# Chain steps in every cell, another softmax for the third unit, and two held pairs of V in a two-block attention kernel

## The chip, the core and the metric

The kernel runs on one core of a Trainium2 chip. The metric is device time in microseconds (us), lower is better. A core has a matmul engine (TensorE, PE in the profile; its weight loads are shown as PEld), a vector engine (VectorE, DVE), an activation engine (ScalarE, ACT), a general engine (GpSimd, POOL) and a queue engine that starts DMAs (SyncE, SP). [...]

## What is computed

Two transformer blocks, one after the other, on x of shape (2, 1024, 256) in fp32, with 16 heads of 16. Both attend to themselves and then to a context of 64 rows for each batch. The first ends with a mixture of 8 experts (two for each row), the second with a plain feed-forward layer. Cut to what matters:

```python
# block 0
q = ln(x);  x = x + mha(q, q)                 # self attention, 1024 keys
x = x + mha(ln(x), ln(ctx))                   # cross attention, 64 keys
h = ln(x);  vals, idx = top_k(h @ rw.T + rb, 2)
x = x + sum_k softmax(vals)[k] * expert[idx[k]](h)   # gelu, 256 -> 1024 -> 256
# block 1
x = x + mha(ln(x), ln(x))
x = x + mha(ln(x), ctx, bias=-10000 * (1 - mask))
x = x + ff(ln(x))                             # gelu, 256 -> 1024 -> 256
```

Each attention is softmax(q k^T / 4) v, with the maximum of each row subtracted.

## The kernel before

**Self attention** of a block (`self_attention`) is a loop over cells. A head group of four heads with 512 queries is eight cells; there are 16 groups (2 batches, 2 halves of the queries, 4 groups of heads), so 128 cells. In cell c four matmuls of kind "a" (L806) make scores for cell c + 10 (`LEAD`) whose row maxima VectorE takes (L813), and four of kind "b" (L817) make the scores of cell c again, transposed and with the maxima subtracted, whose exponentials ScalarE takes (L823). The products with V (`product`, L868) follow every second cell, or a cell alone. `has_a` and `maxima[0]` say that maxima are still to be made: cells 0 to 117. The last cells have "b" alone. The maxima of a group are collected by `collect` (L841), transposed on PE (L714) and subtracted from the queries (L716) in `largest`. `need_heads` forces out, with `stream.until`, the projections of keys and queries (`keys`, `queries`, L636), whose results go through DMAs on SP into the tiles KS and QS, that the next "a" needs.

**All else in the loop** is a task of a planner, `Stream`. A task is a generator: it emits instructions and yields a cost in us of PE time. A cost of zero or less means "not before the next cell" (or so many cells of 2.9 us, `CELL`). A task has a due cell (`last`), a first cell, marks that it waits for (`after`) and a rank. Each cell adds `pace` to an allowance `owed`: at least `RATE`, 2.5 us in block 0 and 1.1 us in block 1, and more when due times need it. Then `stream.step` takes the able task that is due first, and of equals (most have no due time) the one of the highest rank, until the allowance or 3 us are spent. After the loop, `rest` runs what is left by rank, with a model of time for the waits.

**A unit** is 512 rows, of which there are four. When its self attention is finished, `project` adds it to x (two halves, L438 and L446) and calls `when_ready`, which adds the unit's chain by `cross_tasks`: the norm of four row tiles (`norm_task`), the cross attention `weigh` (query projections L1114; then steps), and `share` (the projection). In block 0 the routing of the unit follows (`dispatch_task`: top two experts, places, and eight indirect DMAs on POOL that scatter its rows, L1474), then a search for the experts' tiles (`Mixture.find`), and slots of 256 rows for an expert (`Mixture.slot`). Slot 0 needs the routing of two units, slots 1 to 4 that of three, the others of all four.

**The steps of `weigh`** work on a group g of heads and a row of the group r: scores (SC, L1148), subtraction of the maximum (LA, L1168 and L1169), masks in block 1 (MA), exponentials (EX, L1185), division by the sum (DI, L1191 to L1193), transposes (TU, L1201) and products (PR, L1215). If the unit begins while maxima are made (`whole`), all these are laid out over 19 cells (21 in block 1). Otherwise the exponential is taken as the transposes are copied out, and the sums are made by products: `undivided` (products L1230, sums L1240, reciprocals L1249) and `division` (L1255, L1262). In block 1 the masks are then added by PE (L1139), unless scores were made while maxima are.

**The lead-in** of block 0 makes maxima of ten cells before the loop. At each of its ten points it adds 1.4 us to an allowance; after the eighth it collects the first maxima, fills up with tasks, and transposes them. V is made in four pairs of row tiles (`values`, L606), due in cells 0, 2, 4 and 6.

Of the kernel before, what the change touches and what calls it, by code (L numbers as in the profile page):

```python
# [61 lines left out]
LEAD = 10  # L62
# [59 lines left out]
class Task:  # L122

    def __init__(self, steps, cost, first=-99, last=None, mark=None, after=(), rank=0):
        self.steps, self.left, self.first = steps, cost, first
        self.soft, self.last = last is None, 9999 if last is None else last
        self.mark, self.after, self.rank = mark, after, rank


class Stream:
# [20 lines left out]
    def step(self, cell):  # L153
        while True:
            able = [t for t in self.tasks if t.first <= cell and self.made.issuperset(t.after)]
            if not able:
                return None
            cost = self.advance(min(able, key=lambda t: (t.last, -t.rank)), cell)
            if cost and cost > 0.0:
                return cost  # L160

    def pace(self, cell):

# [39 lines left out]
def two_blocks(  # L203
# [109 lines left out]
    maxima = [True]  # L313
# [163 lines left out]
    whole = tc.dram_tile([NPAIR, 2 * P, 512], F32, name="whole")  # L477
# [49 lines left out]
    def self_attention(layer, tail, heads, arrive, extra, when_ready, beside=None):  # L527
# [89 lines left out]
            free.append(i)  # L617
            yield 2.0

        def add_values(b, first, after):  # L620

            for c0 in range(0, TB, 2):
                stream.add(
                    values(b, c0), 2.0, first=first, last=64 * b + c0, mark=("values", b, c0),
                    after=after if c0 == 0 else [("values", b, c0 - 2)],
                )

# [160 lines left out]
        def project(b, qh, after=()):  # L788
            def go():
                for t0 in range(0, 4, 2):  # L790
                    yield from project_task(ot[b, qh], w, b * TB + 4 * qh + t0, t0, 2)
                when_ready(b, qh, stream, now[0])

            stream.add(go(), 4.0, last=now[0] + 4, rank=60, after=after)

        def score(kind, cell, j):
            h, n = divmod(cell, 8)
# [125 lines left out]
            opool, qpool = results_pool(), weights_pool()  # L923
            stream.made.add(("QB", 0))
        stream.made.update([("norm", 0), ("Q", 0)])
        add_values(0, -99, [("norm", 0)])
        add_heads(2)
        add_heads(4)
        add_heads(6)
# [30 lines left out]
        for cell in range(ncell + 2):  # L960
            now[0] = cell
            ahead = cell + LEAD
            if ahead < ncell and ahead % 16 == 0:
                need_heads(ahead // 8)
            has_a, has_b = ahead < ncell, cell < ncell
            maxima[0] = has_a
            a = [("a", ahead, j) for j in (2, 3, 0, 1)] if has_a else []
            s = [("b", cell, j) for j in range(4)] if has_b else []
            if has_a:
                slot(s[:2] + a[:2])  # L970
                slot(s[2:] + a[2:])
            elif has_b:
                slot(s)
            if ahead % 8 == 7 and has_a:
                h = ahead // 8
                collect(h)
                stream.add(largest(h), 0.75, first=cell + 1, last=cell + 2, mark=("QB", h))
            if (cell + 1) % 8 == 0 and cell + 1 < ncell:
                stream.until(("QB", (cell + 1) // 8))
            for go in later.pop(cell, []):  # L980
                go()
            owed = min(owed, 3.0) + max(stream.pace(cell), 0.0 if has_a else 2.0)
            if cell >= 2 and cell % 2 == 0:
                product([c for c in (cell - 2, cell - 1) if c not in alone])
                if owed < 2.5:
                    continue
            most = 3.0
            while owed > 0.6 and most > 0.0:
                cost = stream.step(cell)
                if cost is None:  # L990
                    break
                owed -= cost
                most -= cost

            if cell % 2 == 1 and most > 2.0 and cell < ncell:
                alone.add(cell - 1)
                product([cell - 1])
# [79 lines left out]
    def cross_tasks(stream, layer, n, pool, first):  # L1077


        att = 2 * layer + 1  # L1080
        w = weights[att]
        b, t0 = n // 2, 4 * n
        name = f"c{layer}{n}"
        held = {}
# [10 lines left out]
        stream.add(  # L1095
            weigh(layer, b, pool, w, name, held), 17.0,
            mark=("weighed", n), after=[("cnorm", n), before[0]], rank=30,
        )
        stream.add(
            share(w, name, t0, held), 5.0, mark=("cross", n),  # L1100
            after=[("weighed", n)], rank=50,
        )

    def weigh(layer, b, pool, w, name, held):

        att = 2 * layer + 1
        kbd, vbd = kbds[layer], vbds[layer]
# [3 lines left out]
        for g in range(2):  # L1111
            i, p = bank()
            for k in range(2):
                nc.tensor.matmul(  # L1114
                    p,
                    lhsT=w[:, X_Q + k * D + g * P : X_Q + k * D + (g + 1) * P],
                    rhs=xT[:, k, :],
                    start=(k == 0),
                    stop=(k == 1),
                )  # L1120
            nc.scalar.activation(
                q[:, g, :], p, AF.Identity, bias=cols[:, C_Q[att] + g : C_Q[att] + g + 1]
            )
            free.append(i)
            yield 1.72
        shape = [P, 4 * 2, SK]
        less, pts, whole_scores = {}, {}, set()


        whole = maxima[0]  # L1130

        def scores(g, n):

# [139 lines left out]
        if whole:  # L1273
# [16 lines left out]
            for now in cells:  # L1290
# [5 lines left out]
                if now is not cells[-1]:  # L1296
                    yield 0.0 if maxima[0] else -1.5
            return
        for step, *args, wait in (
            (SC, 0, 0, None),  # L1300
            (SC, 0, 1, -1.0),
            (TU, 0, 0, None),
            (SC, 1, 0, None),
            (TU, 0, 1, -1.3),
            (undivided, 0, None),
            (SC, 1, 1, None),
            (TU, 1, 0, None),
            (division, 0, None),
            (TU, 1, 1, -1.6),
            (undivided, 1, None),  # L1310
        ):
            step(*args)
            yield costs[step]
            if wait:
                yield wait

    def share(w, name, first, held):

        if held["division"]:
            yield -2.6  # L1320
            held["division"](1)
            yield 0.55
        yield -1.2
        for t0 in range(0, 4, 2):
            yield from project_task(held["ot"], w, first + t0, t0, 2)


    inside = const.tile([P, E], F32, name="inside")
# [869 lines left out]
```

## Time and profile before

| | us |
|---|---|
| median of three runs | 1615.26 (1612.68 to 1616.85) |
| the profiled execution | 1614.59 |
| its span, first to last instruction | 1612.8 |
| PE busy | 1560.5 (97%) |
| DVE busy | 1013.8 (63%) |
| ACT busy | 939.3 (58%) |
| POOL busy | 472.2 (29%) |

By the timeline the span falls into: the lead-in to about 50 us, block 0's loop with maxima to 529, its last cells to 577, the chains of the last units and the first slots to about 656, the other slots to about 948, block 1's loop to 1402, its last cells to 1430, and the rest with the feed-forward layer to the end.

A line of the profile names a line of the kernel, an engine, an operation, and output and inputs by the program's names. A group's line ends with its busy time, the mean of one in ns, and the idle time in front of it with what ended it. In the view of waits the numbers are the total, how often, and the longest. In the page's slices a digit is tenths of a fortieth of the span (40.3 us). PEclk is the granted clock of PE. A matmul in fp32 shows as two records, so a pass of four matmuls has "x8".

### The profile page before, as it was taken

What the parts mean: (1) busy time and instruction counts of PE and PEld (TensorE: products, weight loads), DVE (VectorE), ACT (ScalarE), POOL (GpSimd) and SP (SyncE); (2) the same over time, 40 slices, a digit from 0 to 9 for tenths busy, and PEclk for the clock granted to TensorE, in tenths of its full rate; (3) what the DMA queues carried; (4) which work ended last, traced back from release to release, by engine and by line L of the source; (5) the groups of instructions that cost most, each with busy time, mean ns of one, the idle gap of its engine ahead of it and who ended that gap; (6) DMA issues with size and microseconds to landing.
All of it is one profiled execution on the core that took longest, in us unless ns stands there. A gap on an engine that the chain in (4) does not pass through costs nothing. (4 is left out here: it accounts for less than half of the span.)

```text
span 1612.8 us, 27523 instructions
## 1 busy us (share of the span) xinstructions
PE 1560.5 (97%) x10182; PEld 853.7 (53%) x10182; DVE 1013.8 (63%) x2178; ACT 939.3 (58%) x1821; POOL 472.2 (29%) x589
## 2 busy tenths in 40 slices
PE   7999999999999888899999999999999999999998
PEld 3533443443444356688888753344344444446766
DVE  5788776877878856511114458876777878845400
ACT  3488777866867752332333337876777877864321
POOL 2234333433623302311112032411333525511000
PEclk9899999998999999999999999999999999999999
DMA  5236211100100214475656321101110001000000
GB/s 157 113 134 226 81 34 29 34 14 21 41 25 18 67 49 134 153 272 189 203 190 234 92 73 28 35 21 22 34 34 21 22 27 70 22 28 1 14 13 26
DMA packets 55749, 120.98 MB, mean 75 GB/s; under 512 B 12218, under 2 KB 26428, under 8 KB 55228
## 3 DMA queue, kind: packets, MB, share of 16 engines
q1 hardware_dynamic: 51772, 109.02, 21.0%
q0 software_dynamic: 3456, 9.51, 1.6%
q8 instruction: 82, 1.34, 0.3%
q10 hardware_dynamic: 384, 0.66, 0.2%
q14 instruction: 55, 0.45, 0.1%
HBM read 71.64 MB, written 38.88 MB: 69 GB/s over the span
## 5 line engine op out<-in xcount | busy, mean ns | idle before, releaser
L813 DVE TENSOR_REDUCE mx_s<-banks 128x1 f32<-128x512 f32 x1024 | 633.2, 680 | 187.0 <-PE banks L806 182.5
L823 ACT ACTIVATE pt_s<-banks 128x512 f32<-128x512 f32 x1024 | 532.9, 611 | 134.8 <-PE banks L806 107.0
L806 PE MATMUL banks<-KS,QS 16*128 16x512 f32 x2048 | 535.0, 631 | 0.2 <-issue 0.2
L817 PE MATMUL banks<-qb_s,KS 32*128 32x512 f32 x2048 | 516.5, 624 | 7.2 <-DVE qb_s L716 2.3
L881 POOL TENSOR_TENSOR acc_s<-acc_s,part_s 128x512 f32<-128x512 f32 x151 | 191.6, 1269 | 370.3 <-ACT part_s L880 369.2
L817 PEld LDWEIGHTS banks<-qb_s,KS 32*128 32x128 f32 x2048 | 179.3, 187 | 194.5 <-DVE mx_s L813 116.3
L868 PE MATMUL banks<-pt_s,v_s 128*20 128x512 f32 x2048 | 265.8, 604 | 2.6 <-DVE mx_s L813 1.9
L806 PEld LDWEIGHTS banks<-KS,QS 16*128 16x128 f32 x2048 | 199.1, 185 | 64.9 <-issue 29.5
L1731 PE MATMUL banks<-w_slot,h_s 128*128 128x256 f32 x640 | 145.2, 384 | 0.0
L868 PEld LDWEIGHTS banks<-pt_s,v_s 128*20 128x20 f32 x2048 | 42.4, 98 | 191.7 <-ACT pt_s L823 142.9
L1731 PEld LDWEIGHTS banks<-w_slot,h_s 128*128 128x128 f32 x640 | 121.7, 192 | 20.4 <-DVE mx_s L813 1.5
L1740 DVE SCALAR_TENSOR_TENSOR ys<-banks,gate,b 128x256 f32<-128x256 f32 x40 | 19.3, 483 | 172.0 <-PE banks L1731 167.7
L880 ACT COPY part_s<-banks 128x512 f32<-128x512 f32 x166 | 100.3, 605 | 45.8 <-PE banks L868 41.3
L1746 POOL DMA_INDIRECT results<-ys,to x40 | 38.7, 967 | 261.5 <-DVE ys L1740 183.2
L1707 ACT ACTIVATE h_s<-banks,w_slot 128x256 f32<-128x256 f32 x104 | 43.6, 470 | 111.3 <-issue 64.0
L1701 PE MATMUL banks<-xsT,w_slot 128*128 128x256 f32 x416 | 96.2, 383 | 0.9 <-ACT xsT L377 0.9
L1701 PEld LDWEIGHTS banks<-xsT,w_slot 128*128 128x128 f32 x416 | 78.0, 191 | 15.4 <-DVE mx_s L813 2.3
L636 PE MATMUL banks<-xT_s,w_att 128*128 128x512 f32 x128 | 63.9, 635 | 0.5 <-DVE mx_s L813 0.5
L1864 ACT ACTIVATE h_f<-banks,w_ff 128x512 f32<-128x512 f32 x32 | 22.0, 687 | 69.7 <-PE banks L1861 69.7
L1873 PE MATMUL banks<-w_ff,h_f 128*128 128x256 f32 x256 | 57.3, 380 | 0.0
L1707 ACT ACTIVATE h_s<-banks,spare 128x256 f32<-128x256 f32 x56 | 23.5, 470 | 57.3 <-issue 33.4
L1861 PE MATMUL banks<-hT_f,w_ff 128*128 128x512 f32 x128 | 56.8, 594 | 0.0
(282 smaller groups left out, 1666.0 us busy)
## 6 DMA issues: line engine op xcount, KB each, us to landing
w_slot<-in_ff_w_dram SPq DMA_DIRECT2D x40, 576.0 KB
sorted_rows<-fill SPq DMA_DIRECT2D x36, 520.0 KB
w_slot<-in_ff_w_dram SPq DMA_DIRECT2D x26, 514.0 KB
whole<-acc_s SPq DMA_DIRECT2D x30, 256.0 KB
spare<-in_ff_w_dram SPq DMA_DIRECT2D x14, 514.0 KB
xs<-sorted_rows SPq DMA_DIRECT2D x20, 260.0 KB
y<-results SPq DMA_DIRECT2D x16, 256.0 KB
QS<-stq_s SPq DMA_DIRECT2D x124, 32.0 KB
```

The costliest lines, as they stand in the source:

```text
L636: nc.tensor.matmul(p, lhsT=w[:, at + k * D + pair * P : at + k * D + (pair + 1) * P], rhs=xT[b][:, k, blk * 512 : (blk + 1) * 512], start= ...
L806: nc.tensor.matmul(sc, lhsT=QS[h % 4][r, qc * P : (qc + 1) * P], rhs=K[r, kh * 512 : (kh + 1) * 512], start=True, stop=True,)
L813: return i, lambda: nc.vector.tensor_reduce(mx[h][:, qc, j, kh : kh + 1], sc, AX.X, ALU.max)
L817: nc.tensor.matmul(sc, lhsT=K[r, n * P : (n + 1) * P], rhs=QB[h][r, :], start=True, stop=True)
L823: nc.scalar.activation(pt, sc, AF.Exp, scale=SCALE)
L868: nc.tensor.matmul(o[32 * j : 32 * j + VW, :], lhsT=V[b][:, cell % 8, 4 * g + j, :], rhs=exps.pop((cell, j)), start=(cell == cells[0]), st ...
L880: nc.scalar.copy(part, o)
L881: helper().tensor_tensor(acc[h], acc[h], part, ALU.add)
L1701: nc.tensor.matmul(ph[:, n, :], lhsT=w[:, at : at + P], rhs=xT[:, k, :], start=(k == 0), stop=(k == 1),)
L1707: nc.scalar.activation(h1[:, f, :], ph[:, n, :], AF.Gelu, bias=w[:, W_B1 + f : W_B1 + f + 1])
L1731: nc.tensor.matmul(py, lhsT=h1[:, f, h * P : (h + 1) * P], rhs=w[:, f * D : (f + 1) * D], start=(f == 0), stop=(f == 7),)
L1873: nc.tensor.matmul(py[:, n, :], lhsT=h1[:, f, t * P : (t + 1) * P], rhs=w2[:, f * D : (f + 1) * D], start=(f == 0), stop=(f == 7),)
```

## The change

It has four parts. (1) A task can be `steady`: in every cell with maxima, `go_on` advances all steady tasks as far as they can go, before or in place of the other steps, and what they cost is taken from the allowance. `project` and the tasks of `cross_tasks` become steady; their projections now yield 0.0 between the halves, so that each half has its own cell. (2) The norm of a unit no longer waits for the mark `weighed` of the unit before, but for `asked`, set once that unit's query projections are emitted. (3) In block 0 the third unit takes the path by products (`whole` is false for it), and that path has a layout of eleven steps for the time in which maxima are made. (4) The third and fourth pair of V in block 0 may not be made before cell 6 - LEAD, the one in which the first maxima are collected.

```diff
+    def go_on(self, cell):
+        total = 0.0
+        for t in [t for t in self.tasks if t.steady]:
+            while t in self.tasks and t.first <= cell and self.made.issuperset(t.after):
+                total += max(0.0, self.advance(t, cell) or 0.0)
+        return total
...
-        def add_values(b, first, after):
+        def add_values(b, first, after, held_for=-99):
...
-                    values(b, c0), 2.0, first=first, last=64 * b + c0, mark=("values", b, c0),
+                    values(b, c0), 2.0, first=first if c0 < 4 else max(first, held_for),
+                    last=64 * b + c0, mark=("values", b, c0),
...
                     yield from project_task(ot[b, qh], w, b * TB + 4 * qh + t0, t0, 2)
+                    if t0 == 0:
+                        yield 0.0
...
-            stream.add(go(), 4.0, last=now[0] + 4, rank=60, after=after)
+            stream.add(go(), 4.0, last=now[0] + 4, rank=60, after=after, steady=True)
...
-        add_values(0, -99, [("norm", 0)])
+        add_values(0, -99, [("norm", 0)], 6 - LEAD)
...
                 if owed < 2.5:
+                    if has_a:
+                        owed -= stream.go_on(cell)
                     continue
             most = 3.0
+            going = stream.go_on(cell) if has_a else 0.0
+            owed -= going
+            most -= going
...
-        before = [(m, n - 1) for m in ("cross", "weighed")] if n > 0 else ["context"]
-        stream.add(norm(), 2.0, mark=("cnorm", n), after=before[1:], first=first,
-            rank=67 if layer == 0 else 40)
+        before = ("cross", n - 1) if n > 0 else "context"
+        stream.add(
+            norm(), 2.0, mark=("cnorm", n), after=[("asked", n - 1)] if n > 0 else [], first=first,
+            rank=67 if layer == 0 else 40, steady=True,
+        )
...
-        whole = maxima[0]
+        whole = maxima[0] and (layer, b, held["half"]) != (0, 1, 0)
...
+        if maxima[0]:
+            for now, wait in (
+                (((SC, 0, 0), (LA, 0, 0)), 0.0),
+                (((LA, 0, 1),), 0.0),
+                (((SC, 0, 1), (LA, 0, 2)), 0.0),
+                (((TU, 0, 0), (LA, 0, 3)), 0.0),
+                (((SC, 1, 0), (LA, 1, 0)), 0.0),
+                (((TU, 0, 1), (LA, 1, 1)), 0.0),
+                (((SC, 1, 1), (LA, 1, 2)), 0.0),
+                (((undivided, 0), (LA, 1, 3)), -1.5),
+                (((TU, 1, 0),), None),
+                (((division, 0), (TU, 1, 1)), -1.4),
+                (((undivided, 1),), None),
+            ):
+                for step, *args in now:
+                    step(*args)
+                us = sum(costs.get(step, 0.0) for step, *_ in now)
+                if us:
+                    yield us
+                if maxima[0]:
+                    yield 0.0
+                elif wait is not None:
+                    yield wait
+            return
```

More of the change, by code (lines that the diff above doesn't have):

```diff
@@ L122, with __init__ @@
 class Task:
-    def __init__(self, steps, cost, first=-99, last=None, mark=None, after=(), rank=0):
-        self.steps, self.left, self.first = steps, cost, first
+    def __init__(
+        self, steps, cost, first=-99, last=None, mark=None, after=(), rank=0, steady=False
+    ):
+        self.steps, self.left, self.first, self.steady = steps, cost, first, steady
         self.soft, self.last = last is None, 9999 if last is None else last
@@ L1083, in cross_tasks @@
         name = f"c{layer}{n}"
-        held = {}
+        held = {"half": n % 2}
         def norm():
@@ L1090, in norm @@
                 add_bias(t0, 4, bias_out[1])
-        before = [(m, n - 1) for m in ("cross", "weighed")] if n > 0 else ["context"]
-        stream.add(norm(), 2.0, mark=("cnorm", n), after=before[1:], first=first,
-            rank=67 if layer == 0 else 40)
+        before = ("cross", n - 1) if n > 0 else "context"
         stream.add(
-            weigh(layer, b, pool, w, name, held), 17.0,
-            mark=("weighed", n), after=[("cnorm", n), before[0]], rank=30,
+            norm(), 2.0, mark=("cnorm", n), after=[("asked", n - 1)] if n > 0 else [], first=first,
+            rank=67 if layer == 0 else 40, steady=True,
+        )
+        stream.add(
+            weigh(layer, b, pool, w, name, held, lambda: stream.made.add(("asked", n))), 17.0,
+            mark=("weighed", n), after=[("cnorm", n), before], rank=30,
+            steady=True,
         )
@@ L1100, in cross_tasks, with weigh @@
             share(w, name, t0, held), 5.0, mark=("cross", n),
-            after=[("weighed", n)], rank=50,
+            after=[("weighed", n)], rank=50, steady=True,
         )
-    def weigh(layer, b, pool, w, name, held):
+    def weigh(layer, b, pool, w, name, held, asked):
         att = 2 * layer + 1
@@ L1125, in weigh @@
             yield 1.72
+        asked()
         shape = [P, 4 * 2, SK]
         less, pts, whole_scores = {}, {}, set()
-        whole = maxima[0]
+        whole = maxima[0] and (layer, b, held["half"]) != (0, 1, 0)
         def scores(g, n):
@@ L1298, in weigh @@
             return
+        if maxima[0]:
[11 more added lines that the diff above has]
+                (((undivided, 1),), None),
+            ):
+                for step, *args in now:
[8 more added lines that the diff above has]
+            return
         for step, *args, wait in (
@@ L1325, in share @@
             yield from project_task(held["ot"], w, first + t0, t0, 2)
+            if t0 == 0:
+                yield 0.0
     inside = const.tile([P, E], F32, name="inside")
```

## The prediction

> **What bounds the kernel now.** I read the page's slices first, then busy time by stage, then the waits of the worst stage, then the timelines around them. The matmul engine is busy nearly everywhere, so only the slices below 9, and those with a low clock, can be won.
>
> ```profile
> PE   7999999999999888899999999999999999999998
> PEclk9899999998999999999999999999999999999999
> ```
>
> The low slices are the first two, those from 520 to 680 us, and faintly 1400 to 1440. "Busy" is no proof of full speed[...]. So I also price a stage by its work. A cell (one step of the attention loop) with nothing added repeats at 2.93 us, read from the product that closes it:
>
> ```profile
> 1000.71 1.05 PE L868 MATMUL banks<-pt_s,v_s 128*20 128x512 f32 x8
> 1003.64 1.05 PE L868 MATMUL banks<-pt_s,v_s 128*20 128x512 f32 x8
> ```
>
> The stages that matter, by the windows view (PE, PEld, DVE, ACT, POOL busy us; granted clock; DMA):
>
> ```profile
> core 0: us, PE busy (x) PEld busy (x) DVE busy (x) ACT busy (x) POOL busy (x), PEclk, DMA share, GB/s
> 529.00:577.00 48.00, 41.27 (x296) 15.97 (x289) 36.43 (x86) 36.51 (x73) 11.81 (x12) 0.93 0.26 88
> 577.00:656.00 79.00, 62.83 (x401) 46.73 (x401) 51.40 (x181) 26.35 (x52) 19.14 (x21) 0.92 0.30 101
> 1402.00:1430.00 28.00, 27.52 (x206) 10.54 (x204) 13.51 (x36) 24.36 (x49) 3.86 (x4) 1.00 0.03 11
> 1430.00:1446.00 16.00, 12.70 (x64) 5.16 (x58) 8.67 (x25) 8.78 (x17) 7.53 (x16) 0.89 0.16 51
> ```
>
> 529 us is the last matmul for maxima (L806) in layer 0, 1402 the one in layer 1. The cells left then have exponentials only: 48 us in layer 0, 28 us in layer 1. From 577 to 656 layer 0 waits for chains: 16.2 us of PE idle, and what waits says why:
>
> ```profile
> PE banks L370 <- DVE xd_m L1364: 6.5, 1, 6.5
> PE banks L370 <- DVE xn_c L358: 3.6, 2, 1.9
> PE banks L1240 <- issue: 3.1, 6, 1.1
> PE banks L370 <- DMA ctx<-in_ctx_dram: 2.2, 1, 2.2
> PE banks L817 <- DVE begin L1520: 2.2, 1, 2.2
> PE banks L868 <- DVE mx_s L813: 1.9, 1, 1.9
> ```
>
> xd_m is the routing (dispatch) of the fourth unit, xn_c the norm of its cross attention: latency with too little matmul work ready beside it. The expert slots 1 to 4 could be that work, but need the third unit's routing, whose first scatter (L1474) the timeline has at 619.5 us, since the third unit's cross attention ends only with its residual add at 589.3.
>
> [...] this trace has a 64-column VectorE operation at 2.93 us where the next of that form takes 0.23:
>
> ```profile
> 534.01 2.93 DVE L1493 TENSOR_TENSOR has<-count,cols 128x64 f32<-128x64 f32 x1
> 537.30 0.23 DVE L1493 TENSOR_TENSOR has<-count,cols 128x64 f32<-128x64 f32 x1
> 542.07 0.67 DVE L716 TENSOR_TENSOR qb_s<-QS,banks 128x512 f32<-128x512 f32 x1
> ```
>
> The last line is the last head's maxima; PE waits for them at 542.8.
>
> **The change, part by part.** Cell numbers come from the code; I place them in the trace by the divisions (L509): in layer 0 cell 102 at 459.8 us.
>
> *Two pairs of V held.* The lead-in is bound by VectorE (maxima back to back from 36.9 to 49.3 us). Following the allowance by hand (1.4 us a step), the third pair changes places with the bias products: both are a few matmuls, 1.75 and about 2.1 us. The fourth pair stands before the transposes already. The 1.1 us wait for L841 there stays. Cost 0; bounds -5 and +3, because 53 to 67 us runs at half clock and a shift of a microsecond may move that.
>
> *Steady chains, layer 0.* Before, the units' query projections (L1114) start at 245, 369 and 509 us, by my cells about 52, 81 and 113; taken every cell they fall on 48, 80 and 111. A gain of three cells, no saved work: 0. The bound below is VectorE: four maxima take 2.48 of 2.93 us, and a cell that adds a subtraction's reduce (0.68) and a division's (0.68 + 0.20) needs 4.04. Such cells exist before too, since a unit could go one step a cell; I take +3 for tighter packing over both layers, range 0 to +8.
>
> *Third unit by products.* Out: 8 exponentials in place on ACT (0.65 each), 8 divisions (0.68 + 0.20 DVE, 1.04 POOL or 0.69 DVE). In: on PE two sums (L1240, 0.87 for 32 matmuls in the chain view) and two spreads (L1255, about 1.0), 3.8 us, plus two reciprocals (0.95) and two multiplies (0.68) on DVE. The old path has 19 steps of a cell, the new one 11, several of them in one cell. From cell 111 it runs to about 125, inside the loop; before, its tail of steps and its projection ran after 577.
>
> - Loop with maxima (bound by PE): one score pair (1.06) and two transposes (1.09 each) come in: +3.
> - 529 to 577: the ten cells left hold 40 exponentials at 2.06 us for four (20.6 us); with the copies that is some 33 us of ACT, and 48 are spent. Half of the stall around 529 to 545 is routing and search of the second unit meeting the last maxima; these come only three cells earlier. The third unit's divisions leave DVE. I take -6 of the 15, bounds 0 and -15.
> - 577 to 656: the last product (1.1) and projection (3.6) are gone, -4.7; the sums and spreads are charged, +3.8. Routing of the third unit can start some 20 us earlier (about 570 for 589.9), so the slots' 14 us apiece (68 records at 193 per 40 us in 720 to 760) are there from about 615 instead of 643. Of the 16.2 us idle I take 11 as filled and 2 us of half-clock time. What is late next is the fourth unit's own chain, which no edit shortens. Sum -14, bounds -3 and -22.
>
> *Steady chains, layer 1.* Here the chains lag: cross attention of unit 0 is projected at 1290 us, of unit 1 at 1418, after the loop, and unit 2 begins only at 1440. Taken every cell, unit 1 ends at about cell 103 and unit 2 begins at 112 of the 118 with maxima, so it takes the path by whole scores. That takes work off PE, from these rows of 1430 to 1525 us, half of which are unit 2's:
>
> ```profile
> L1139 PE MATMUL banks<-mask_i,ones 1*128 1x128 f32 x128 | 12.9, 282 | 0.0
> L1240 PE MATMUL banks<-pt_c,picks 128*32 128x128 f32 x128 | 4.2, 273 | 0.0
> L1255 PE MATMUL banks<-inv_c,picks 128*128 128x128 f32 x32 | 4.2, 275 | 0.0
> ```
>
> Sums 1.75, spreads 1.75, and masks of the two score pairs that still run with maxima, about 0.9 each as they overlap the scores: -5.3. The idle of 1430 to 1446 (3.3) and its half clock (0.11 x 16 = 1.8) go, since the feed-forward norms are ready. Everything else of units 1 and 2 moves from the tail into the loop, both bound by PE: no gain. Against it, 1402 to 1430 is bound by ACT (24.4 of 28 busy), and about five exponentials of 0.65 come in: +3.5. Sum -7, bounds -12 and -2.
>
> *What the steady steps displace.* They are charged to the allowance, 1.1 us a cell in layer 1, that pays for head projections. Around cell 48 a unit takes 4.4 us at once; by hand the queries for head 8 then get only as far as their projection by cell 53 and are forced out at 54. Their eight DMAs stand on SP in front of the next maxima. At the start a head takes 3.3 us from eviction (20.7) to the first matmul that waits for it (24.06). One such wait: +4, bounds 0 and +30.
>
> **The sum**, against this execution's 1614.59 us (span 1612.8, 0.7 us below the median of 1615.26): 0 + 3 + 3 - 6 - 14 - 7 + 4 = -17, so 1598 us.
>
> **Rivals.**
> - *Slower: late heads in layer 1.* Six head tasks fall under running chains there (K and Q of heads 8 and 10, Q of 12 and 14). Each forced one costs 3.3 us and may bring half clock as at 392 to 400, about 3 us more: 6.3. Without any the sum is -21. Four late ones give 1619, five 1625: from five on it is slower than before. For it: the low rate; against it: the pace rises as a due time nears, and there are four cells between due and need.
> - *No gain: the idle only moves.* Slots arrive earlier but the fourth unit's chain sets the end, and early idle returns between 656 and 690. Then -3 in place of -14, and 0 in place of -6: about 1614 less what layer 1 keeps, 1613.
> - *More: everything fills.* 529 to 577 falls to what ACT needs (-15), all idle goes (-22), no late head: 1614.6 + 6 - 15 - 22 - 7 = 1577.
> - *Unit 2 doesn't start in time.* If its weights begin after cell 117 in layer 1, that layer keeps -3 at most: 1602. This counts with the forecast.
>
> **How the numbers follow.** Forecast 0.53 (its own range 1588 to 1607), everything fills 0.17, no gain 0.12, late heads 0.18. About 0.3% (4.8 us) is what a measurement can tell from no change. Faster 0.70, same 0.12, slower 0.18. The range reaches to four late heads above and nearly to the full gain below: 1579 to 1619.
>
> **What would show it.** Right: the first scatter of unit 2 about 20 us earlier; PE idle between the end of layer 0's maxima and full slots falling from some 23 to below 12 us; in layer 1 unit 2's L1114 before the last L806, and L1139 down to about 96 records. Wrong: waits of L806 or L817 on DMAs of KS or QS in layer 1; the 2.93 us cells stretched by DVE; new half-clock stretches inside the loops.

## The result, and the profile after

The changed kernel takes 1629.8 us (median of four, 1627.4 to 1633.3) against 1616.1 for the kernel before in the same session: a ratio of 1.009, with a 95% interval from 1.007 to 1.012. It is slower by some 14 us, where 17 less were forecast. The profiled execution has 1633.29 us, with a span of 1631.5.

A line of the kernel before is found in the changed one some 10 to 50 lines lower: the maxima's matmul L806 is L820 now, L817 is L831, the product L868 is L882, the maxima's reduction L813 is L827, the unit's query projection L1114 is L1137, its scores L1148 are L1173, the subtraction L1168 is L1193.

The slices of the page first, answering to those of before:

```profile
PE   7999999999999999999999999999899999999998
PEclk9799999999999899999999999999899999999999
```

The 8s after the first loop are gone, so the stretch from 520 to 680 us is filled as intended. In their place there is one 8, at about 1170 us, with a clock of 8 in the same slice; another clock of 8 stands at about 550 us. The rest of the loss can't be seen here. It needs the windows, cut by the last maxima (561 and 1443 us), by the last product of block 0 (603) and the last scores of block 1 (1475), and by the first full slots (680) and block 1's loop (962). The columns are as before: length, busy time of PE, PEld, DVE, ACT and POOL, clock, DMA share, GB/s.

```profile
72.00:561.00 489.00, 480.22 (x3352) 203.77 (x3352) 369.07 (x709) 345.94 (x670) 189.06 (x232) 0.97 0.17 57
561.00:603.00 42.00, 41.81 (x339) 17.59 (x332) 22.54 (x64) 29.94 (x59) 1.25 (x2) 0.94 0.10 33
603.00:680.00 77.00, 71.52 (x474) 55.04 (x474) 49.68 (x175) 31.94 (x64) 21.52 (x24) 0.98 0.42 153
680.00:962.00 282.00, 276.96 (x1336) 230.55 (x1337) 92.72 (x331) 85.92 (x193) 46.61 (x47) 1.00 0.53 176
962.00:1443.00 481.00, 469.90 (x3390) 201.15 (x3392) 359.88 (x647) 347.79 (x666) 191.31 (x232) 0.99 0.12 33
1443.00:1475.00 32.00, 31.74 (x279) 13.59 (x272) 21.05 (x36) 30.52 (x63) 5.96 (x5) 1.00 0.03 10
1475.00:1631.00 156.00, 150.90 (x757) 102.23 (x752) 45.99 (x98) 45.51 (x73) 11.00 (x32) 1.00 0.06 19
```

The kernel before, with the same cuts (its last product of block 0 ends at 569 us; the 577 of the prediction takes in 8 us more):

```profile
72.00:529.00 457.00, 453.16 (x3316) 193.84 (x3312) 364.05 (x697) 340.35 (x662) 179.20 (x223) 0.99 0.18 59
529.00:569.00 40.00, 35.50 (x248) 12.13 (x241) 32.48 (x75) 32.33 (x66) 11.33 (x12) 0.91 0.16 56
569.00:656.00 87.00, 68.60 (x449) 50.58 (x449) 55.35 (x193) 30.53 (x60) 19.62 (x22) 0.93 0.34 114
948.00:1402.00 454.00, 449.39 (x3308) 191.00 (x3308) 347.82 (x617) 338.40 (x650) 172.99 (x192) 1.00 0.12 35
```

Against before: block 0's loop with maxima 489 for 457 us, its last cells 42 for 40, from there to block 1's loop 359 for 379; block 1's loop 481 for 454, its last cells 32 for 28, the end 156 for 183. In block 0 the loop loses 32 us, and 18 come back behind it. In block 1 the loop takes 27 us more and its last cells 4, and the end 27 less, since work of the end was moved into the loop.

The waits of PE from 594 to 680 us, answering to those of 577 to 656 before (total, times, longest):

```profile
PE banks L381 <- DVE xd_m L1415: 3.3, 2, 2.1
PE banks L1226 <- DVE sc_c L1194: 0.9, 2, 0.6
PE banks L1137 <- ACT xT_c L388: 0.5, 1, 0.5
PE banks L1489 <- DVE before_m L1481: 0.3, 1, 0.3
```

16 us of idle PE (23 from the last maxima on) have become 5.5 (6), as hoped: the routing of the fourth unit (xd_m) still shows, the rest is covered. The groups of 1455 to 1550 us have fewer masks, and the sums and spreads of one unit fewer, as the prediction had it (12.9, 4.2 and 4.2 us before):

```profile
L1164 PE MATMUL banks<-mask_i,ones 1*128 1x128 f32 x96 | 9.6, 278 | 0.0
L1265 PE MATMUL banks<-pt_c,picks 128*32 128x128 f32 x64 | 2.1, 273 | 0.0
L1280 PE MATMUL banks<-inv_c,picks 128*128 128x128 f32 x16 | 2.1, 275 | 0.0
```

And a plain cell of block 1 repeats at 2.92 us, as before (start, duration):

```profile
1011.26 1.05 PE L882 MATMUL banks<-pt_s,v_s 128*20 128x512 f32 x8
1014.18 1.05 PE L882 MATMUL banks<-pt_s,v_s 128*20 128x512 f32 x8
```

So the gains came, and a plain cell costs what it did. The loops lost time in cells that aren't plain, and PE counts as busy in nearly all of it.

### The profile page after: what moved, and what is told of

Read it like the earlier page. It is cut to its first block, busy times and chain, and to the rows that moved or that the text cites. A ratio compares the mean times of both kernels' runs of the same rounds, so it can differ in the third digit from the quotient of the medians.

```text
span 1631.5 us, 27471 instructions
## 1 busy us (share of the span) xinstructions
PE 1585.1 (97%) x10150; PEld 856.3 (52%) x10150; DVE 1007.3 (62%) x2157; ACT 940.5 (58%) x1824; POOL 485.2 (30%) x615
## 5 line engine op out<-in xcount | busy, mean ns | idle before, releaser
L827 DVE TENSOR_REDUCE mx_s<-banks 128x1 f32<-128x512 f32 x1024 | 634.7, 682 | 195.2 <-PE banks L820 172.7
L820 PE MATMUL banks<-KS,QS 16*128 16x512 f32 x2048 | 553.7, 638 | 6.5 <-DMA QS<-stq_s 4.4
L831 PE MATMUL banks<-qb_s,KS 32*128 32x512 f32 x2048 | 523.9, 630 | 9.0 <-DVE mx_s L827 4.6
L831 PEld LDWEIGHTS banks<-qb_s,KS 32*128 32x128 f32 x2048 | 182.7, 189 | 188.9 <-DVE mx_s L827 111.5
L882 PE MATMUL banks<-pt_s,v_s 128*20 128x512 f32 x2048 | 272.1, 615 | 0.6 <-ACT pt_s L837 0.5
L820 PEld LDWEIGHTS banks<-KS,QS 16*128 16x128 f32 x2048 | 202.8, 188 | 82.6 <-issue 35.7
L882 PEld LDWEIGHTS banks<-pt_s,v_s 128*20 128x20 f32 x2048 | 43.0, 99 | 196.1 <-ACT pt_s L837 142.3
L1194 POOL TENSOR_TENSOR sc_c<-sc_c,mx_c 128x512 f32<-128x512 f32 x42 | 43.8, 1044 | 62.4 <-DVE mx_c L1193 55.7
```

Of the source, the lines that this page charges most:

```text
L820: nc.tensor.matmul(sc, lhsT=QS[h % 4][r, qc * P : (qc + 1) * P], rhs=K[r, kh * 512 : (kh + 1) * 512], start=True, stop=True,)
L827: return i, lambda: nc.vector.tensor_reduce(mx[h][:, qc, j, kh : kh + 1], sc, AX.X, ALU.max)
L831: nc.tensor.matmul(sc, lhsT=K[r, n * P : (n + 1) * P], rhs=QB[h][r, :], start=True, stop=True)
L882: nc.tensor.matmul(o[32 * j : 32 * j + VW, :], lhsT=V[b][:, cell % 8, 4 * g + j, :], rhs=exps.pop((cell, j)), start=(cell == cells[0]), st ...
```

## Experiments

Times are medians. For each run the table gives the ratio to the kernel before, run on the same chip (the chips differ: its medians are 1610.9 to 1617.3 us, up to 0.4% apart), and four stretches of its profiled execution: block 0's loop, from its first to its last collection of maxima (L855); from there to block 1's first; block 1's loop; and what follows to the end of the span.

| run | us | ratio, interval | loop 0 | between | loop 1 | end |
|---|---|---|---|---|---|---|
| before | 1616.1 | | 484.4 | 406.6 | 464.0 | 208.5 |
| changed | 1629.8 | 1.009 (1.007 to 1.012) | 514.1 | 389.9 | 492.8 | 185.1 |
| changed again (e17) | 1630.1 | 1.009 (1.007 to 1.011) | 508.9 | 387.7 | 497.3 | 188.3 |
| e1 no steady steps | 1601.4 | 0.991 (0.989 to 0.993) | 487.1 | 390.5 | 474.4 | 197.6 |
| e2 steady in block 1 | 1613.3 | 0.998 (0.997 to 0.999) | 490.3 | 392.5 | 494.5 | 186.7 |
| e3 steady in block 0 | 1622.7 | 1.004 (1.003 to 1.005) | 509.2 | 387.9 | 474.4 | 197.6 |
| e4 fewer even cells | 1613.8 | 0.998 (0.997 to 0.999) | 505.8 | 387.9 | 480.2 | 187.9 |
| e5 one step a cell | 1604.1 | 0.991 (0.989 to 0.993) | 494.3 | 395.6 | 475.3 | 192.1 |
| e6 the same, block 1 only | 1606.0 | 0.993 (0.991 to 0.994) | 489.6 | 394.7 | 475.5 | 194.7 |
| e7 e1 with V as before | 1604.1 | 0.991 (0.988 to 0.993) | 491.4 | 395.3 | 474.8 | 198.0 |
| e8 e2, heads due earlier | 1605.0 | 0.992 (0.990 to 0.994) | 490.3 | 392.3 | 487.1 | 186.8 |
| e9 e1 with bursts | 1604.2 | 0.992 (0.990 to 0.994) | 491.2 | 389.1 | 476.8 | 195.5 |
| e10 e6, heads due earlier | 1603.7 | 0.991 (0.989 to 0.994) | 490.5 | 392.7 | 475.5 | 195.1 |
| e11 e1 without products | 1614.6 | 0.999 (0.998 to 1.000) | 487.9 | 403.6 | 472.3 | 196.0 |
| e12 e5, heads due earlier | 1603.6 | 0.992 (0.990 to 0.994) | 490.6 | 389.4 | 478.0 | 195.1 |
| e13 changed, cheaper maximum | 1620.1 | 1.007 (1.005 to 1.008) | 503.9 | 380.7 | 497.9 | 185.4 |
| e14 e1, cheaper maximum | 1586.4 | 0.985 (0.984 to 0.987) | 484.0 | 380.9 | 473.3 | 197.6 |
| e15 steady in odd cells | 1601.6 | 0.995 (0.993 to 0.996) | 495.4 | 385.7 | 481.2 | 187.9 |
| e16 routing held | 1641.4 | 1.018 (1.015 to 1.020) | 503.5 | 408.0 | 491.8 | 185.1 |
| e18 e10, cheaper maximum | 1600.7 | 0.990 (0.988 to 0.992) | 486.6 | 393.9 | 475.8 | 196.1 |

The stretches come from one execution each. e1, e2, e6, e8 and e10 have the same program up to block 1 and show 487.1 to 490.5 in loop 0 and 390.5 to 394.7 after it, so some 4 us of a stretch are no effect.

### Which part costs: the steady steps, in which block

The two calls of `go_on` are switched off (e1), or left in one block (e2: `layer == 1`, e3: `layer == 0`). e4 drops only the first of the two.

```diff
-                    if has_a:
+                    if has_a and False:
                         owed -= stream.go_on(cell)
...
-            going = stream.go_on(cell) if has_a else 0.0
+            going = stream.go_on(cell) if has_a and False else 0.0
```

The theories have letters in the expectations, which stand here as written before each run.

> The changed kernel with both calls of go_on switched off: the third unit still goes by products and the V pairs are still held, but chain steps are again taken only as the allowance permits. Changed kernel 1630, kernel before 1616. Theory A (the loss of 32 us in layer 0's loop comes from the steady steps, which load VectorE cells that are already full): the loop with maxima falls from 489 us back to about 460, and the total to 1604-1614, because the b-only stage keeps part of its gain. Theory B (the loss is the late heads in layer 1): layer 1 returns to its 454 us, layer 0 keeps 489: about 1624. Theory C (the product path of the third unit is what stretches the loop): the loop stays at 485-490 and the total at 1625-1632.

> The changed kernel with go_on in layer 1 alone. Theory A (layer 0's steady steps cost): layer 0's loop about 460 us, layer 1 as in the changed kernel, total 1605-1615, clearly below the changed kernel's 1630. Theory B (late heads in layer 1): total 1624-1630, layer 0 loop near 489 or not, since the loss stays. Theory C (products): 1625-1632.

> The changed kernel with go_on in layer 0 alone. Theory A: layer 0 as in the changed kernel (loop 489 us), layer 1 as before, total 1624-1630. Theory B (late heads in layer 1): no wait of the first maxima of a head on the queries' DMA in layer 1, total 1612-1620. Theory C: as A here.

> The changed kernel without the go_on call in even cells, where a product has just been issued and the allowance is below 2.5; in odd cells and where the allowance suffices the steady steps stay. Theory E (the steps in even cells make matmul bursts beside the products, so that the maxima's VectorE starves in that cell and the matmuls wait in the next): most of the 32 us in layer 0's loop goes, loop 465-472, total about 1612-1618. Theory A in its narrow form (VectorE work of the steps itself, wherever it is put): the same VectorE work at nearly the same time, so the loop stays at 480-489, total 1622-1630.

Without steady steps the rest of the change is a gain of 15 us on the kernel before. Steady steps cost 21 us in block 0 (e3 against e1) and 12 in block 1 (e2 against e1); together 33, where the changed kernel shows 28. Theory A holds against C, though e1 and e3 end a little below its ranges (1604 and 1624). B holds only for block 1's share. e1 is also faster than both kernels. Its loops, by the windows view:

```profile
72.00:533.00 461.00, 456.31 (x3323) 194.44 (x3322) 364.51 (x705) 341.75 (x664) 187.94 (x231) 0.99 0.18 60
934.00:1398.00 464.00, 458.72 (x3345) 193.72 (x3337) 353.88 (x634) 344.76 (x661) 179.66 (x209) 0.99 0.12 35
```

461 us for nearly the records that take 489 in the changed kernel (3323 against 3352). e4 gave 16 us back, but its loop 0 (480 us from 72 us on, 506 in the table) isn't at the 465 to 472 expected; loop 1 gains more (480 for 493), and there no maxima wait for queries any more (see the late heads below).

### The V pairs, and the products

e7 is e1 with `add_values(0, -99, [("norm", 0)])` as before. e11 is e1 with `whole = maxima[0]` as before.

> The changed kernel without steady steps and with the third and fourth pair of V where they were: the product path of the third unit is what is left of the change. Against 1601 with the V pairs held. If the V edit costs nothing, 1599-1604; if holding V removes half-clock time at the start (the granted clock of the first 72 us is 0.91 there against 0.88 before), 1603-1607; if it costs, 1596-1599.

> Without steady steps (base 1601) and with the third unit of layer 0 back on whole scores; what is left of the change is the order of the norms and of some waits, and the V pairs. If the products' path is the gain of 15, as the prediction's terms of layer 0 have it (+3 -6 -14 = -17): 1613-1618. If the gain is the earlier norm (it waits for the unit before to have asked, no longer for its weights): 1600-1605.

e7's 1604.1 against 1601.4 lies within the intervals, so the V edit can't be told from nothing. e11 gives up 13 us, all of it between the loops (403.6 against 390.5): the path by products is the gain. The first scatter of the third unit comes at 597.5 us in e1 and at 620.8 in e11. e11 still has the earlier norm (part 2 of the change) and the held V, and takes what the kernel before takes (0.999), so these are worth nothing by themselves. Whether the earlier norm matters beside steady steps wasn't tried.

### Bursts

In the changed kernel VectorE idles long wherever a unit starts. PE's weight loads and VectorE's timeline from 236 to 246 us show one (start, duration, then in brackets the idle time before it):

```profile
239.61 0.30 PEld L1137 LDWEIGHTS banks<-xT_c,w_att 128*128 128x128 f32 x2 [0.85 <-DVE mx_s L827]
243.24 0.97 PEld L1173 LDWEIGHTS banks<-kbd,q_c 32*128 32x128 f32 x16 [0.76 <-issue]
```

```profile
236.78 2.48 DVE L827 TENSOR_REDUCE mx_s<-banks 128x1 f32<-128x512 f32 x4 [0.54 <-PE banks L820]
245.05 0.69 DVE L1193 TENSOR_REDUCE mx_c<-sc_c 128x8 f32<-128x512 f32 x1 [5.79 <-ACT sc_c L1184]
```

Two products, both halves of the query projection and the first score pair fall into one cell, since `go_on` goes on through costed steps. VectorE has no maxima for 5.8 us. e5 lets each task take one step with a cost in a cell; e6 does so with steady steps in block 1 alone.

```diff
             while t in self.tasks and t.first <= cell and self.made.issuperset(t.after):
-                total += max(0.0, self.advance(t, cell) or 0.0)
+                cost = max(0.0, self.advance(t, cell) or 0.0)
+                total += cost
+                if cost > 0.0:
+                    break
```

> The changed kernel with go_on taking at most one step with a cost per task and cell, in both layers; before, it went on through every step that had no wait behind it, so a unit's query projection (twice 1.72) and its first score pair fell into one cell. Theory E (bursts: VectorE has no maxima to take while the projections run, and the matmuls wait for it in the next cells): VectorE's idle time in front of the chain's own maxima (L1193 behind the copy L1184) falls from 36 us to 11-18, layer 0's loop from 490 to 463-472, layer 1's wait of the maxima behind L831 from 18 to below 8, total 1603-1613. Theory A in its narrow form (the chain's VectorE work packed into consecutive cells): it is packed as before, so loop 480-490 and total 1622-1630.

> As the run before, but steady steps in layer 1 alone. Base for it: 1613 with unlimited steps in layer 1, 1601 with none. Theory E: the 13 us of VectorE idle behind L831 go for the most part; with the late head's wait left (4 to 6 us) about 1601-1607; if the tail then keeps its 20 us gain, below 1601. Theory A narrow: 1610-1615.

e5 gives 26 of the 28 us back, and all its numbers fall where theory E had them. VectorE's waits for the chain's scores, from 72 to 530 us (to the end of the loop it is 36), in the changed kernel, then in e5 (where this line of code is L1196):

```profile
DVE mx_c L1193 <- ACT sc_c L1184: 24.5, 8, 6.9
```

```profile
DVE mx_c L1196 <- ACT sc_c L1187: 14.0, 8, 2.5
```

That looked like a proof. So the burst was also put alone into e1: the two costs of a unit's query projection are not yielded but added to that of its first score pair, so that it falls into one cell, and nothing else is hurried.

```diff
             free.append(i)
-            yield 1.72
         asked()
+        owing = [3.44]
...
-                us = sum(costs.get(step, 0.0) for step, *_ in now)
+                us = sum(costs.get(step, 0.0) for step, *_ in now) + (owing.pop() if owing else 0.0)
```

> Without steady steps (base 1601), but each unit's query projection, both halves, and its first score pair made one step of 4.4 us that falls into one cell; nothing else is hurried. Theory E (the burst itself costs, since VectorE gets no maxima meanwhile): VectorE shows an idle of 5 to 7 us at each unit that starts inside a loop (three in layer 0, two in layer 1) as in the changed kernel, some 2 to 4 us more of time for each, total 1607-1620. Rival (the burst is harmless and the cost is the count of hurried cells): 1599-1605.

It costs 2.8 us, with intervals that overlap. By the order of the matmuls two of block 0's three bursts stand in cells with two products (80 and 112), as in the changed kernel, and VectorE's timeline has such a gap at the second unit:

```profile
373.44 0.69 DVE L1193 TENSOR_REDUCE mx_c<-sc_c 128x8 f32<-128x512 f32 x1 [6.19 <-ACT sc_c L1184]
```

Theory E falls: a burst of projections by itself isn't what costs. Letting one step through per cell must help by something else that it changes.

### Cell by cell

VectorE's first maximum of each cell is in the trace of every run, so each cell can be timed. From the order of the matmuls in the trace I counted each cell's matmul work: 1.88 us (a plain 2.93 less its product), 1.05 for each product, 3.44 for a unit's query projections (eight records 0.43 us apart), 1.0 for a score pair, about 1.1 for a pair's transposes, and so on; these are estimates from how long such groups take in the traces. VectorE's work is the time in which it was busy between two such maxima. The last two columns are for the cells that a half-clock stretch touches: the half-clock time, and by how much these cells are longer than their larger part. For cells 46 to 116 of block 0, where the chains run, in us:

| run | time | matmul work | VectorE work | sum of each cell's larger one | half clock | time beyond the larger one there |
|---|---|---|---|---|---|---|
| before | 304 | 278 | 245 | 301 | 10 | 1 |
| changed | 331 | 280 | 246 | 306 | 30 | 14 |
| changed again | 326 | 280 | 246 | 306 | 17 | 8 |
| e4 | 326 | 280 | 247 | 308 | 17 | 9 |
| e5 | 314 | 279 | 248 | 299 | 24 | 8 |
| e15 | 314 | 279 | 248 | 307 | 14 | 2 |
| e9 | 311 | 279 | 243 | 305 | 10 | 3 |
| e12 | 308 | 279 | 244 | 298 | 7 | 2 |
| e1 | 306 | 279 | 243 | 300 | 7 | 1 |
| e16 | 322 | 279 | 248 | 308 | 20 | 3 |
| e13 | 322 | 280 | 239 | 304 | 14 | 5 |
| e14 | 303 | 279 | 234 | 296 | 3 | 1 |

The matmul work is the same in all of them, and VectorE's in the first nine nearly so. (The last three rows belong to the next part.) What differs is how it is dealt out. In these runs a cell without half clock lasted about as long as its larger part (0.3 us off on average), so by this count a cell full of matmuls beside one full of VectorE work costs more than two mixed ones. Unequal cells give 6 to 7 us of the 25 and 20 by which the two executions of the changed kernel stand above e1, and their growth comes in cells 70 to 85 (4 us) and 102 to 116 (3 us). In cells touched by half clock another 13 and 7 us are added. The rest, 5 and 6 us, is spread over the other cells and not explained. So uneven cells alone don't make the loss: e15 has as high a sum as the changed kernel and takes 12 to 17 us less, and e5's 8 us above e1 all go with the half clock. Windows of the changed kernel (columns as above) in front of two half-clock stretches and in them:

```profile
366.00:378.00 12.00, 9.39 (x60) 3.95 (x52) 11.66 (x26) 7.92 (x16) 5.10 (x4) 1.00 0.01 2
378.00:385.00 7.00, 6.81 (x32) 2.54 (x32) 5.12 (x12) 2.17 (x4) 0.00 (x0) 0.51 0.00 0
512.00:525.00 13.00, 9.68 (x62) 4.50 (x54) 12.65 (x30) 8.30 (x16) 5.03 (x4) 0.99 0.00 1
525.00:532.00 7.00, 7.00 (x36) 3.01 (x35) 4.85 (x14) 2.38 (x5) 0.00 (x0) 0.53 0.00 1
```

VectorE is busy 97% of 12 and 13 us, PE 78% and 74%; just before the clock halves PE has waited 1.9 and 1.6 us for VectorE's maxima. The half clock then lies on the scores and the two products of cells 80 and 112. The next unit's projections (L1137) follow at 385.5 and 532.4 us, at full clock. Why the clock halves just there isn't shown. What VectorE does in front of the first of them is in its timeline from 364 to 371 us:

```profile
364.54 2.49 DVE L827 TENSOR_REDUCE mx_s<-banks 128x1 f32<-128x512 f32 x4 [3.34 <-PE banks L820]
367.16 1.68 DVE L369 TENSOR_SCALAR xn_c<-x_sb,mv_c,rs_c 128x256 f32<-128x256 f32 x2
369.20 1.03 DVE L1452 TENSOR_TENSOR hot_m<-lg_m,mx_m 128x32 f32<-128x32 f32 x1
370.27 0.19 DVE L1453 TENSOR_TENSOR hot_m<-hot_m,desc 128x32 f32<-128x32 f32 x1
```

The norm of the second unit (xn_c) and the routing of the first (hot_m) stand in the same cells, 77 and 78, which last 6.3 and 6.6 us with 3.3 and 4.1 of matmul work; cell 80, with the two products and the projections, lasts 10.6. In e1 the norm has cells 77 and 78 (4.3 us each) and the routing's own VectorE work comes in cells 82 to 86. The same happens at cells 109, 110 and 112.

### Taking VectorE work out of the loop

Two edits bear on it. The cheaper maximum, in the changed kernel (e13) and in e1 (e14), is taken over 8 of the 64 keys in block 0:

```diff
-            nc.vector.tensor_reduce(mx, src, AX.X, ALU.max)
+            nc.vector.tensor_reduce(mx, src[:, :, :8] if layer == 0 else src, AX.X, ALU.max)
```

> The changed kernel, with the maximum that is subtracted from layer 0's cross scores taken over the first 8 of 64 keys (a shift that the softmax divides out again), so that each of 24 reductions of 0.68 us on VectorE becomes some 0.2 us. Base 1630. Theory F (a cell lasts as long as the larger of its matmul and its VectorE work, and the steady steps set these into different cells): the reductions lie in cells without matmul steps, so most of 24 x 0.48 = 11.5 us comes back: 1618-1624. Bursts or half clock alone: at most 3 us: 1626-1630.

> The same cheaper maximum without steady steps. Base 1601. Theory F: part of the reductions lies beside matmul steps there, so less comes back, 2 to 6 us: 1595-1600, and the gap to the run before (28 us without it) shrinks to 20-25. If VectorE is no bound in these cells: 1600-1603 and the gap stays.

> Steady steps in both layers, unlimited in number, but in odd cells only (even where the allowance would permit one in an even cell, go_on isn't called). By the order of the instructions the chains then run two to four cells later than in the changed kernel and meet fewer of the cells with two products. If cells with two products and a step are what counts: 1602-1608. If the early start of chains and of the routing behind them (VectorE work of routing and of the next norm in the same cells) is: 1602-1610 too, but with the head of 8 cells around cell 78 back at some 31-36 us. If neither: 1614 or more, as with odd cells preferred (1614).

In the trace the reductions take 0.21 for 0.68 us. Loop 0 falls to 503.9 from 514.1 and 508.9 in the changed kernel, and to 484.0 from 487.1 to 490.5 without steady steps, so the loops agree with theory F, weakly. But cells 77, 78, 109 and 110 have none of these reductions and stay at 6.3, 6.6, 5.3 and 6.4 us. In the cells above the sum of larger ones falls by 2 us, in e14 by 4, where theory F expects the larger fall in e13; the half clock falls too (14 us for 30 and 17). The totals don't agree: the ratios are 1.007 and 0.985, so the gap between the two is 2.1%, where it was 1.8%, not the smaller one expected. In both the stretch between the loops is 9 us shorter, which I hadn't counted; e18, with the same block 0 as e14 on another chip, doesn't show it (393.9). What the cheaper maximum is worth stays open.

e15 calls `go_on` in odd cells alone (`if has_a and cell % 2 == 1`, and not in the other place). Its ratio of 0.995 lies between e5 and e4. Loop 0 takes 495 us, so having no steps in even cells gives back part of the loss. The sum of larger ones, 307, hasn't fallen; what has is the time in half-clock cells and the unexplained rest. The groups of eight cells around cell 78 stay at 38 and 42 us, not 31 to 36.

In e16 all chain steps stay in their cells, and only the routing is held for four cells. Its first part, the norm of the routed rows, thereby falls into cells 77 and 78, where the next unit's norm is, so the two aren't parted there as intended:

```diff
+        if maxima[0]:
+            yield -4 * CELL
         mv, rs = yield from statistics(src, 4, name)
```

> The changed kernel with a unit's routing held four cells (11.6 us) after its cross attention while maxima run in layer 0; by the order of the instructions all chain steps stay in their cells, and the routing of unit 0 moves from cells 75-82 to 79-86, that of unit 1 from 106-115 to 110 and later. Theory G (routing and the next norm load VectorE in the same cells, 6.3 and 6.6 us in cells 77 and 78, 5.3 and 6.4 in 109 and 110): those four cells fall to about 4.3 us each, 6 to 8 us less in the loop with what the routing costs elsewhere taken off, the ratio to the kernel before falls from 1.009 to 1.004-1.006. Theory E or the half clock alone (projection bursts): 1.007-1.010.

> The changed kernel once more, on the chip of the run before, so that the two compare without the difference between chips: all theories, a ratio to the kernel before of 1.007-1.0115.

Loop 0 falls by 5 to 11 us (503.5), about as theory G has it, but cells 77, 78, 109 and 110 take 5.8, 5.8, 5.8 and 3.9 us, not 4.3 each, and the sum of larger ones doesn't fall. But the total rises by 11, and the expectation is missed: the stretch between the loops is 408.0 for some 389. Windows behind the loop, of the changed kernel and of e16:

```profile
562.00:680.00 118.00, 112.33 (x807) 72.63 (x806) 71.22 (x235) 61.25 (x121) 22.56 (x25) 0.97 0.31 111
```

```profile
551.00:680.00 129.00, 116.14 (x777) 74.32 (x772) 73.64 (x250) 57.53 (x114) 28.42 (x31) 0.91 0.31 104
```

With the routing late, the third unit's last scatter comes at 643.9 us for 630.6, and there are 13 us of idle PE for 6, and a clock of 0.91. Holding the routing moves the stall; keeping the chains from being hurried removes it.

### The late heads of block 1

e8 is e2 with block 1's head tasks due earlier; e10 and e12 add this to e6 and e5. e18 is e10 with the cheaper maximum.

```diff
-            last = 8 * h - LEAD - 4
+            last = 8 * h - LEAD - 4 - 4 * layer
```

> Steady steps in layer 1 alone, unlimited, with the head tasks of layer 1 due four cells earlier. Base 1613. Theory B (the late queries of one head, 5.6 us of wait and some half-clock time after it): the wait of L820 on QS goes, total 1603-1608. Theory E: the wait goes or moves, and at most 5 us with it: 1608-1613, since the bursts stay.

> One costed step per task and cell, in layer 1 alone, with layer 1's head tasks due four cells earlier: both remedies together. If burst and late heads are two separate costs of layer 1 (1613 with both, 1606 and 1605 with one remedy each), then 1597-1601, at or below the kernel without steady steps (1601). If each remedy removes the same wait, 1604-1607.

> One costed step per task and cell in both layers, with layer 1's head tasks due four cells earlier. Base 1604 without the earlier heads. If the late head is a cost of its own there (the wait of L820 on QS): 1599-1602. If one step a cell leaves no late head any more: 1602-1606.

> What helped, together: the third unit by products, no steady steps in layer 0, one costed step a cell and head tasks four cells earlier in layer 1, and the cheaper maximum in layer 0. Base: the cheaper maximum without any steady steps, ratio 0.985. If the two remedies for layer 1 add something to it: 0.980-0.984; if not, as the runs without the cheaper maximum have it (1604 against 1601): 0.985-0.989.

The first maxima of a head wait for its queries in the changed kernel, and in e2 (matmul, idle time before it):

```profile
1175.80 2.85 PE L820 MATMUL banks<-KS,QS 16*128 16x512 f32 x7 [4.36 <-DMA QS<-stq_s]
```

```profile
1155.96 2.85 PE L820 MATMUL banks<-KS,QS 16*128 16x512 f32 x7 [5.58 <-DMA QS<-stq_s]
```

In e8 no such wait is left, nor in e4 and e15; loop 1 has 487.1 for 494.5 us, and the total is 8 us less. In e6 the wait is gone too without the earlier dues, and loop 1 has 475.5. So the two remedies largely remove the same wait, and e10 is no better than e6. No version with steady steps is faster than e1, and e18 (0.990) misses both of its expectations. The fastest run of all is e14, e1 with the cheaper maximum.

## Why the prediction was wrong

- *V held, 0 (bounds -5 to +3).* Nothing that e7 can tell from 0.
- *Third unit by products: +3 -6 -14 = -17 in block 0.* The size was nearly right: 13 us (e11 against e1). The first scatter of that unit came 22 us earlier without steady steps (597.5 for 619.5), as named; in the changed kernel it came at 621.7, since the loop before it had grown. From the last maxima to block 1's loop the changed kernel takes 18 us less, where -6 and -14 make -20, and idle PE there fell as said (23 to 6 us up to the full slots). How -6 and -14 share it can't be read: the cut at 577 has no like in the changed kernel.
- *Steady chains, block 0: "0 and +3 for tighter packing on DVE over both layers (0 to +8)".* This is the step that failed: it measured +21 (e3 against e1). I priced a VectorE-heavy cell by one reduction and one division, and held that such cells exist before too. I looked at each task alone. The steady rule moves the end of one unit's chain forward, and with it the routing behind it, into the cells of the next unit's norm; it then puts two products and a whole query projection into one cell. Before, routing and norm hardly met (cells 77 and 78), and the sum of a cell's larger part grew by 6 to 7 us at equal work. Half clock adds more, 13 and 7 us in the cells it touches: the prediction named it as a sign, not as a cost. The "gain of three cells" holds for the first unit alone: by the order of the matmuls the projections stood in cells 51, 80 to 81 and 112 before, and stand in 48, 80 and 112 now.
- *Steady chains, block 1: -7, with late heads +4.* The end gained (185 us for 208 before), the sums and spreads fell by 2.1 us each for 1.75 forecast, and the third unit began in the loop. Yet e2 is 12 us above e1. The late head is the larger part, 8 us (e8), for one head and not the five that the rival needed. It came where the prediction had put it, at head 8 around cell 48, but at twice the price.
- *The rivals.* "Late heads" gave the right sign by a mechanism that exists and is the smaller loss. The larger one, cells stretched by VectorE and half clock in the loop, stood only in the list of signs, without a price. ("No gain" sums to 1615, not 1613.)

Shown: the loss is the steady steps', 21 us in block 0 and 12 in block 1; the products bring 13; one costed step a cell or none removes nearly all the loss; in block 1 most of it is one late head. Supported, not proved: how it comes about in block 0. By the cells' times it is 6 to 7 us of unequal cells, 7 to 13 us more in cells touched by half clock, and 5 to 6 us unexplained. No edit took one of these away alone, e13 and e16 left routing and norm together in cells 77 and 78, and their totals didn't follow. That VectorE's load brings on the half clock is a guess from two places.

## What to carry to other kernels

Where two engines share a loop's cells, add up the larger of their two loads cell by cell (here a cell without half clock was 0.3 us off the larger one on average), and do this for the new order, with the work that the moved step pulls along behind it; then look for new half-clock stretches. A rule that hurries a chain did no harm here when it took one costed step a cell, and no good either. A repair that helps when added isn't a proof of the cause: put the suspected cause in alone as well.

## What was not expected of the hardware

In a half-clock stretch the granted clock is 0.50 (378.01 to 384.84 us in the changed kernel). In the traces of both kernels these stretches last 3.4, 6.8, 10.2, 13.7 or 17.1 us, steps of 3.41, but for one at the very end of each trace. PE was at work in front of them: in 512 to 525 us of the changed kernel it was busy for 9.7 of 13 us. In the 3.41 us right before its stretches at 378.0 and 524.8 us PE was busy for 1.71 and 1.80 us, before those at 419.0 and 552.1 us for 2.95 and 3.34. In the kernel before, the stretch that the prediction puts at 392 to 400 us lasts from 391.46 to 401.70; in the 3.41 us in front of it PE was busy for 2.02 and idle for 1.39. The half-clock time in cells 46 to 116 was 30 and 17 us in two executions of the changed kernel.

The comparison L1452 above took 1.03 us where the next operation of its form took 0.19. GpSimd worked from 368.92 to 370.18, and the operation ended just after, at 370.23:

```profile
368.92 1.26 POOL L441 TENSOR_TENSOR x_sb<-x_sb,bias_out 128x512 f32<-128x512 f32 x1 [0.23 <-DVE xn_c L369]
```

The operation of 2.93 us that the prediction shows (534.01 to 536.94) ended just after the last of three of GpSimd's, one behind the other (536.85):

```profile
533.59 1.05 POOL L1193 TENSOR_TENSOR sc_c<-sc_c,sm_c 128x512 f32<-128x512 f32 x1
534.59 1.26 POOL L881 TENSOR_TENSOR acc_s<-acc_s,part_s 128x512 f32<-128x512 f32 x1
535.81 1.04 POOL L1169 TENSOR_TENSOR sc_c<-sc_c,mx_c 128x512 f32<-128x512 f32 x1
```

VectorE's operation ended 0.05 us after GpSimd's in the one place and 0.09 us in the other. What made it long isn't shown.
